# Two first-layer attentions on shared buffer rings, with the start of the second moved beside the end of the first

## The chip, the cores and the metric

The kernel runs on one core of a Trainium2 chip, in one launch. The metric is the device time of the launch in microseconds (us). Before the change three runs took 2728.13, 2721.87 and 2728.06 us; their median is 2728.06 us.

## The reference

A small vision transformer: a convolutional tokenizer turns 128 images of 128x128 into 64 tokens of 256 features each, and then two pre-norm layers follow. Only the two attentions of the first layer matter here.

```python
h = tokenizer(x)                                   # [128 images, 64 tokens, 256 features]
h = h + relu_attention(layernorm(h))               # 1: 8 heads of 32 features
h = h + expert_attention(layernorm(h))             # 2: 4 experts, 4 feature chunks, 2 heads of 32
h = h + linear_attention(layernorm(h))             # layer 1
h = h + experts(layernorm(h))                      # layer 1, gated, 8 experts

def relu_attention(x):      # a score is a small MLP over the positive part of (query - key)
    q, k, v = x @ Wq.T, x @ Wk.T, x @ Wv.T
    scores = relu(relu(q[:, None] - k[None]) @ w_mlp + b_mlp)    # per head
    return softmax(scores) @ v

def expert_attention(x):    # normalizes once more, inside
    residual = x
    xn = normalized(x) * norm_w
    gate = softmax(xn @ router_w.T + router_b)                   # over 4 experts
    q, k, v = xn[chunk] @ qkv_w[expert]
    y = softmax(q @ k.T / sqrt(32)) @ v
    y = (y @ proj_w[expert] + proj_b[expert]) weighted by gate
    return residual + y @ out_w
```

All data is fp32. The residual stream stays in SBUF for the whole first layer, in the tile `h2` of 128 partitions (2 images x 64 tokens) by 64 "pairs" of images by 256 features.

## The kernel before, in words

**First attention** (`relu_attention`, lines 290 to 757). The 128 images are cut into 8 blocks of 16 images; a block has 64 queries per image, taken 8 at a time, so there are 64 chunks (0 to 63), 8 per block. The order in which every engine gets its instructions is written out by hand (`tc.manual_schedule`): one loop body per chunk, with named places (O, X, A, V1, Y, B, W, V2, C, Z, in this order) where a dictionary `work` hangs further steps. A place belongs to one engine for the most part: O, A, B and C hold ScalarE copies, X, Y and Z matmuls, V1 and V2 VectorE steps, W GpSimd steps. In the chunk's own body VectorE makes maxima of queries and keys (L517), GpSimd makes differences (L525) that ScalarE rectifies (L526), ScalarE makes some parts alone (L535), and TensorE sums all these parts over the features of a head into the scores `sc` (L327). Beside a chunk runs the softmax of the chunk before it (VectorE L551 to L553, ScalarE L558, VectorE L561 and L562, GpSimd L565), its transpose on TensorE (L574) and the copy of that by ScalarE into the tile `at` (L582). The dictionary hangs the next block's preparation beside these chunks (statistics L347, factors L357 and L358, normalization L375, transposes L384 and L390, keys L396, values L415), and the end of the block before: `outcome`, weights times values (L471), its copies (L482), `back`, a transpose (L489), and `added`, the addition to `h2` (L499). Chunks 56 to 63 belong to the last block; no further block is prepared beside them.

After chunk 63 the last chunk's softmax and the last block's end run alone, with some idle matmuls (`c.busy`, L49) between them. Then all SBUF and PSUM pools of the first attention close.

**Second attention** (`expert_attention`, lines 760 to 1097). It opens pools of its own (L770 to L776), loads eight weight tensors (L779 to L799), multiplies two of them together (L811, kept at L819), and then runs a loop over the 64 pairs. Four pairs form a block. A block needs statistics (L834, L835), nine small GpSimd steps that make factors (`factors`, L843 to L851), per pair one GpSimd step for the normalized tile (L857) and one that normalizes `h2` in place (L860), two transposes (L865, copied at L870), router logits (L876) and their softmax (L883 to L895). In the loop these run some pairs ahead (statistics 11 and 10 pairs ahead, factors 9, transposes 4 and 3); for block 0, and in part for blocks 1 and 2, ahead means before the loop (`do("first")`, L1054, outside the manual schedule). A pair needs queries and keys (L918, copied at L922), values (L932; one half copied by ScalarE at L941, one half by VectorE with a bias at L943), scores (L954), their softmax (L966, L967, L970, L973, L974, L980, L981), the transposes of its weights (L990, L993), the product with the values (`mixed`, L1003, L1011) and the output (L1017, L1018). Every fourth pair's result leaves for DRAM (L1020). Pair p's transposes and output run in the iteration of pair p+1, and in iteration p the queries, keys and values of pair p+1 are made. Buffers: queries and keys 2, values 3, PSUM for everything but scores 4, PSUM for scores 2 of two banks each.

PSUM has 8 banks. The first attention uses 2 for scores, 2 for queries, 3 for everything else (`apq`) and 1 for the transposed weights of a chunk (`apt`); the second uses 4 for scores and 4 for the rest.

Of the kernel before, what the change touches and what calls it, by code (L numbers as in the profile page):

```python
# [1 line left out]

# [9 lines left out]
F32 = mybir.dt.float32  # L12
# [7 lines left out]
P = 128  # L20
# [269 lines left out]
def relu_attention(c, wqkv, wmlp, bmlp):  # L290
# [7 lines left out]
    NP = NB // 2  # L298
    with (
        tc.tile_pool(name="aw", bufs=1) as wp,  # L300
        tc.tile_pool(name="an", bufs=2) as np_,
        tc.tile_pool(name="ab", bufs=2) as bp,
        tc.tile_pool(name="aat", bufs=1) as atp,
# [3 lines left out]
        tc.tile_pool(name="ae", bufs=2) as ep,  # L307
        tc.tile_pool(name="aps", bufs=2, space=PSUM) as pss,
        tc.tile_pool(name="apc", bufs=2, space=PSUM) as psc,
        tc.tile_pool(name="apq", bufs=3, space=PSUM) as psq,  # L310
        tc.tile_pool(name="apt", bufs=1, space=PSUM) as pst,
    ):
        w = wp.tile([P, 2, 3 * D], F32, name="w")
# [21 lines left out]
        class Block:  # L335
# [41 lines left out]
            def transpose(self, i):  # L377

                if i == 0:
                    self.xT = bp.tile([P, 2, NP, P], F32, tag="xT", name="xT")  # L380
                self.ps["x", i] = pt = psq.tile([P, 2, 2, P], F32, tag="pq", name="pt")
                for fc in range(2):
                    for n in range(2):
                        nc.tensor.transpose(  # L384
                            pt[:, fc, n], self.xn[:, 2 * i + n, fc * P : fc * P + P], c.ident
                        )
# [5 lines left out]
            def keys(self, s, fo):  # L392

                self.ps["k", s, fo] = pk = psq.tile([P, 8, T], F32, tag="pq", name="pk")
# [15 lines left out]
            def values(self, i):  # L410

                self.ps["v", i] = pv = psq.tile([P, 2, D], F32, tag="pq", name="pv")
# [15 lines left out]
            def key_sums(self):  # L428
                self.ps["b"] = pk = psq.tile([P, T], F32, tag="pq", name="pkb")
# [34 lines left out]
            def outcome(self, hf):  # L464
                self.ps["o", hf] = po = [psq.tile([P, NP, T], F32, tag="pq", name="po") for _ in range(2)]
# [13 lines left out]
            def outcome_copied(self, hf, par):  # L479
                if hf == 0 and par == 0:  # L480
                    self.oT = np_.tile([P, 2, NP, 2, T], F32, tag="oT", name="oT", bufs=1)
                nc.scalar.copy(self.oT[:, hf, :, par], self.ps["o", hf][par])  # L482

            def back(self, i):

                self.ps["h", i] = pt = psq.tile([P, 2, D], F32, tag="pq", name="pto")
# [14 lines left out]
        class Chunk:  # L501
# [65 lines left out]
            def transpose(self):  # L567


                self.pt = pt = pst.tile([P, 8, 64], F32, tag="pt", name="pt")  # L570
# [50 lines left out]
        for b, x in enumerate(blocks):  # L621
            n = 8 * b

            at(n + 9, "X", of(x.outcome, 0))
            at(n + 9, "A", of(x.outcome_copied, 0, 0))
            at(n + 9, "B", of(x.outcome_copied, 0, 1))
            at(n + 9, "Y", of(x.outcome, 1))
            at(n + 9, "C", of(x.outcome_copied, 1, 0))
            at(n + 10, "O", of(x.outcome_copied, 1, 1))
            for i in range(4):  # L630
                at(n + 10 + i // 2, "XY"[i % 2], of(x.back, i))
                at(n + 10 + (i + 1) // 2, ("V2", "V1")[i % 2], of(x.added, i))
# [48 lines left out]
            at(n, "B", of(x.valued, 3))  # L681

# [4 lines left out]
        with tc.manual_schedule():  # L687
# [61 lines left out]
            old.exponents()  # L749
            old.sums()  # L750
            old.weights()
            c.busy(psq.tile([P, 8, T], F32, tag="pq", name="idle"), blocks[-1].k[:, 0, 0:8], 5)
            old.transpose()
            old.transposed()
            for n in range(len(seq), len(seq) + 12):
                for place in ("O", "X", "A", "V1", "Y", "B", "V2", "C", "Z"):
                    do(n, place)
        assert not work


def expert_attention(c, hd, normw, wr, br, wqkv, wvT, wproj, bproj, wout):
# [7 lines left out]
    with (  # L769
        tc.tile_pool(name="fw", bufs=1) as wp,  # L770
        tc.tile_pool(name="fb", bufs=3) as bp,
        tc.tile_pool(name="fn", bufs=2) as np_,
        tc.tile_pool(name="fv", bufs=3) as vp,
        tc.tile_pool(name="fe", bufs=4) as ep,
        tc.tile_pool(name="fps", bufs=2, space=PSUM) as pss,
        tc.tile_pool(name="fpq", bufs=4, space=PSUM) as psq,  # L776
    ):
        nw = wp.tile([P, 2], F32, name="nw")
        nc.sync.dma_start(nw, normw)  # L779
        wrs = wp.tile([P, 2, 4], F32, name="wrs")  # L780
        nc.sync.dma_start(wrs, wr.rearrange("(c p) e -> p c e", p=P))
        brs = wp.tile([P, 4], F32, name="brs")
        nc.sync.dma_start(brs, br.partition_broadcast(P))
        w = wp.tile([P, 2 * D], F32, name="w")


        bv = wp.tile([P, P], F32, name="bv")
        for k in range(2):
            nc.sync.dma_start(w[k * 64 : k * 64 + 64, :], wqkv)
            nc.sync.dma_start(  # L790
                bv[k * 64 : k * 64 + 64, :],
                bproj[2 * k : 2 * k + 2].rearrange("e o -> (e o)").partition_broadcast(64),
            )
        wv = wp.tile([32, 8, 64], F32, name="wv")
        nc.scalar.dma_start(wv, wvT)
        wpj = wp.tile([32, 8, 64], F32, name="wpj")
        nc.scalar.dma_start(wpj, wproj)
        wo = wp.tile([P, 2, D], F32, name="wo")
        nc.scalar.dma_start(wo, wout.rearrange("(c p) n -> p c n", p=P))  # L799
        eps = wp.tile([P, NB], F32, name="eps")  # L800
# [1240 lines left out]
```

## Time and profile before

| | us |
|---|---|
| median of three runs | 2728.06 |
| the profiled execution's own time | 2725.85 |
| its span (first to last instruction) | 2724.2 |
| last matmul of chunk 63 (L327) ends | at 1097.4 |
| last addition of the first attention (L499) starts its group | at 1110.7 |
| first scores of the second attention (L954), pair 0 | at 1137.46 |
| scores of pair 1 | at 1148.72 |
| scores of pair 63, the last | at 1902.09 |

Times in the trace count from the start of the span. Busy time is the time in which an engine executes at least one instruction. TensorE has two rows: PE is matmuls, PEld is the loading of weights. A matmul in fp32 shows as two records. PEclk is the granted share of TensorE's full clock. "Idle before" of a group is how long its engine stood still before its instructions, and the arrow names what ended the wait.

### The profile page before, as it was taken

How to read it: one execution, taken by the hardware profiler on the slowest of the kernel's cores; microseconds unless marked ns; L12 is line 12 of the kernel's file. 1: busy time of each engine (PE TensorE's matmuls, PEld its weight loads, DVE VectorE, ACT ScalarE, POOL GpSimd, SP SyncE). 2: the span in 40 equal slices, each digit the busy share in tenths (PEclk: the TensorE clock that was granted, in tenths of full speed). 3: DMA queues.
4: the chain of work that ended last, by engine and by line, in shares of the span. 5: the costliest groups of instructions: out<-in, count | busy, mean ns of one | idle time of the engine just before them, and what ended most of it. 6: DMA issues, size and time to landing. Idle time of an engine off the chain costs nothing. (4 is left out here: it accounts for less than half of the span.)

```text
span 2724.2 us, 80786 instructions
## 1 busy us (share of the span) xinstructions
PE 2574.9 (95%) x35209; PEld 1749.1 (64%) x35209; DVE 2023.0 (74%) x3024; ACT 1619.3 (59%) x3398; POOL 1632.4 (60%) x1386
## 2 busy tenths in 40 slices
PE   8989999999999999799999999999799996999997
PEld 4553444444444443588888888888466565888886
DVE  5759999999998999478777787877367676444443
ACT  2228888888888888466666666666255543223332
POOL 3328888888888889666566666553233312455444
PEclk9999999999999999899999999999899998999998
DMA  3100000000000000000000000000424444555554
GB/s 110 32 12 1 2 1 2 1 2 2 1 2 1 2 2 1 13 11 11 19 11 19 11 11 19 11 19 12 117 63 106 101 110 153 178 192 196 188 193 133
DMA packets 137998, 141.13 MB, mean 52 GB/s; under 512 B 107603, under 2 KB 121429, under 8 KB 129952
## 3 DMA queue, kind: packets, MB, share of 16 engines
q1 hardware_dynamic: 126896, 118.00, 14.5%
q0 software_dynamic: 7648, 14.77, 1.7%
q8 instruction: 278, 4.55, 0.7%
q10 hardware_dynamic: 3088, 3.08, 0.4%
q14 instruction: 88, 0.72, 0.1%
HBM read 104.03 MB, written 32.54 MB: 50 GB/s over the span
## 5 line engine op out<-in xcount | busy, mean ns | idle before, releaser
L525 POOL TENSOR_TENSOR m<-q,k 128x1024 f32<-128x1024 f32 x384 | 719.0, 1904 | 31.5 <-PE sc L327 16.3
L517 DVE TENSOR_TENSOR m<-pc,k 128x2048 f32<-128x2048 f32 (+1 forms) x320 | 646.8, 2058 | 0.5 <-ACT q L461 0.5
L327 PE MATMUL sc<-m,wide 128*32 128x512 f32 x4096 | 529.8, 599 | 12.0 <-DVE m L517 7.1
L526 ACT ACTIVATE m<-m 128x1024 f32<-128x1024 f32 x384 | 402.3, 1049 | 5.9 <-POOL m L525 5.4
L327 PEld LDWEIGHTS sc<-m,wide 128*32 128x32 f32 x4096 | 126.9, 109 | 259.4 <-issue 146.0
L535 ACT ACTIVATE m<-k,q 128x64 f32<-128x64 f32 x1024 | 270.9, 339 | 0.8 <-DVE k L408 0.8
L966 DVE TENSOR_REDUCE mx<-sc 128x16 f32<-128x1024 f32 x128 | 156.1, 1220 | 144.8 <-PE sc L954 142.4
L981 POOL TENSOR_TENSOR e<-e,mx 128x1024 f32<-128x1024 f32 x128 | 243.5, 1903 | 10.1 <-POOL mx L980 0.2
L922 ACT COPY qk<-pqk 128x512 f32<-128x512 f32 x256 | 139.0, 605 | 136.7 <-PE pqk L918 136.7
L980 POOL TENSOR_TENSOR mx<-mx,gate 128x16 f32<-128x16 f32 x128 | 27.6, 216 | 294.9 <-ACT z L1011 149.0
L1871 PE MATMUL ph<-xt,w1s 128*128 128x256 f32 x896 | 198.8, 380 | 3.8 <-DVE xt L1862 2.3
L1887 PE MATMUL po<-w2s,hT 128*128 128x256 f32 x896 | 198.0, 379 | 0.0
L993 ACT COPY pT<-pt 128x512 f32<-128x512 f32 x256 | 138.8, 599 | 92.1 <-PE pt L990 92.1
L1871 PEld LDWEIGHTS ph<-xt,w1s 128*128 128x128 f32 x896 | 170.0, 190 | 28.2 <-DVE xt L1862 3.0
L1887 PEld LDWEIGHTS po<-w2s,hT 128*128 128x128 f32 x896 | 168.3, 190 | 21.5
L918 PE MATMUL pqk<-xT,w 64*128 64x128 f32 x2048 | 169.9, 289 | 3.7 <-issue 3.5
L967 DVE TENSOR_TENSOR e<-sc,mx 128x1024 f32<-128x1024 f32 x128 | 156.8, 1225 | 4.4
L1905 POOL DMA_INDIRECT out<-y,rout x56 | 56.7, 1013 | 167.8 <-ACT hT L1875 124.8
L918 PEld LDWEIGHTS pqk<-xT,w 64*128 64x128 f32 x2048 | 142.3, 189 | 21.8 <-issue 11.8
L973 DVE TENSOR_REDUCE mx<-e 128x16 f32<-128x1024 f32 x128 | 153.2, 1197 | 1.8 <-ACT e L970 1.8
L990 PE MATMUL pt<-ident,e 128*128 128x128 f32 x1024 | 144.0, 281 | 11.1 <-DVE v L943 5.1
L1875 ACT ACTIVATE hT<-ph,w1s 128x256 f32<-128x256 f32 x224 | 93.0, 470 | 96.9 <-PE ph L1871 96.9
(298 smaller groups left out, 4926.5 us busy)
## 6 DMA issues: line engine op xcount, KB each, us to landing
w1s<-in_we SPq DMA_DIRECT2D x30, 1028.0 KB, 5.1
w2s<-in_we SPq DMA_DIRECT2D x30, 1024.0 KB, 4.9
hd<-h SPq DMA_DIRECT2D x16, 512.0 KB, 3.2
x<-hd SPq DMA_DIRECT2D x16, 512.0 KB, 3.8
h<-hd SPq DMA_DIRECT2D x4, 2048.0 KB, 13.2
hx<-h SPq DMA_DIRECT2D x4, 2048.0 KB, 11.6
out<-h SPq DMA_DIRECT2D x4, 2048.0 KB, 20.5
xt<-in_x SPq DMA_DIRECT2D x15, 512.0 KB, 3.6
```

The lines of the kernel that those rows point to most:

```text
L327: nc.tensor.matmul(dst[j : j + 32], wide[:, hf, s : s + 32], part, start=start, stop=stop)
L517: nc.vector.tensor_tensor(m, bcast(self.pq[:, hf, i : i + n], 3, T), k, ALU.max)
L525: nc.gpsimd.tensor_tensor(m, bcast(self.q[:, hf, s : s + 2], 3, T), k, ALU.subtract)
L526: nc.scalar.activation(m, m, AF.Relu)
L535: nc.scalar.activation(self.parts[i, hf][:, q], self.blk.k[:, hf, i], AF.Relu, bias=self.q[:, hf, i - NB // 2, q : q + 1], scale=-1.0,)
L918: nc.tensor.matmul(pq[par][:, k, eh, :], w[r, f : f + P], self.xT[r, fc], start=True, stop=True)
L966: nc.vector.tensor_reduce(mx, sc, AX.X, ALU.max)
L967: nc.vector.tensor_sub(e, sc, bcast(mx, 2, T))
L973: nc.vector.tensor_reduce(self.sm[x], self.e[x], AX.X, ALU.add)
L981: nc.gpsimd.tensor_mul(e, e, bcast(sm, 2, T))
L1871: nc.tensor.matmul(ph[:, j], self.w1[:, w0 : w0 + P], self.xt[:, fc], start=(fc == 0), stop=(fc == 1))
L1887: nc.tensor.matmul(po, self.hT[:, f, r * P : r * P + P], self.w2[:, f, :], start=(f == 0), stop=(f == 7))
```

## The change

1. A class `Shared` holds the pools that both attentions use: one ring of 4 PSUM banks for everything but scores and queries (in the first attention it takes the place of the 3 of `apq` and the 1 of `apt`), and the SBUF rings of the first attention. The second attention has no SBUF pools of its own but for softmax tiles (`fe`); it takes slots of the first's rings: queries and keys from the ring `k`, values from the ring `v` (2 slots, where its own had 3), weights from a slot of `xT`, and three "rows" (`xn`, the other `xT`, `oT`), each of which holds a block's normalized tile in one half and its transpose in the other.
2. `expert_attention` is called first; it returns a dictionary `beside` of steps and a function `rest`. `relu_attention` hangs the steps of `beside` into its chunks: statistics of the second attention's blocks 0, 1 and 2 beside chunks 43 to 48; factors of blocks 0 and 1, cut in four parts each, beside 45 to 52; the weights' loads at 55 and 57, now all on SyncE's queue; the product of two of them at 58; block 0's normalization, on ScalarE (`normal_scalar`) where GpSimd did it, at 58 and 59; its transposes, logits and gates at 59 to 63; queries, keys and values of pair 0 at 61 to 63. The small loads of `normw`, the router's weight and bias move to the start of the first attention.
3. The end of the last chunk and of the last block no longer runs before the second attention. A function `first` writes out the order of pair 0 by hand, with the last chunk's softmax and transpose, `outcome`, `back` and `added` among pair 0's own steps; two of the outcome's four copies go to VectorE. The in-place normalization of block 0 (`stream`) comes last in it on GpSimd, that of block 1 beside pairs 2 and 3. The idle matmuls are gone.
4. From pair 1 on the loop is as before, but for block 2, whose factors come two pairs later than its distance would have them (at pair 1) and whose normalization comes at pairs 1, 2, 3 and 3.

```diff
+class Shared:
+    def __init__(self, c, ctx):
+        self.np_, self.bp = pool("an", 2), pool("ab", 2)
+        self.atp, self.ep, self.small = pool("aat", 1), pool("ae", 2), pool("as", 1)
+        self.psq = pool("apq", 4, space=PSUM)
...
-        tc.tile_pool(name="apq", bufs=3, space=PSUM) as psq,
-        tc.tile_pool(name="apt", bufs=1, space=PSUM) as pst,
...
+        for (n, place), steps in beside.items():
+            at(n, place, *steps)
...
             old.less_max()
-            old.exponents()
-            old.sums()
-            old.weights()
-            c.busy(psq.tile([P, 8, T], F32, tag="pq", name="idle"), blocks[-1].k[:, 0, 0:8], 5)
-            old.transpose()
-            old.transposed()
-            for n in range(len(seq), len(seq) + 12):
-                for place in ("O", "X", "A", "V1", "Y", "B", "V2", "C", "Z"):
-                    do(n, place)
+    return old, blocks[-1]
...
+    def ring(pool, tag, shape, **k):
+        t = pool.tile(shape, F32, tag=tag, name=f"{tag}r", **k)
...
+        def load(self):
+            row = ring(sh.bp, "xT", [P, 2, 8, P])
...
+        def load_values(self):
+            for k, x in enumerate((wvT, wproj)):
+                y = sh.w[0:32, k, D : 3 * D].rearrange("p (e n) -> p e n", e=8)
+                nc.sync.dma_start(y, x)
...
+        def offsets(self):
+            g.tensor_mul(self.nb, self.mv[:, 0:NB, 0], self.ra)
+            g.tensor_scalar(self.nb, self.nb, -1.0, None, ALU.mult)
...
+        def stream(self, n):
+            nc.gpsimd.tensor_scalar(hn, hn, self.rs[:, i], self.mr[:, i], ALU.mult, ALU.subtract)
+        def normal_scalar(self, n):
+            nc.scalar.activation(self.xn[:, n, :], hn, AF.Identity, bias=self.nb[:, i], scale=self.ra[:, i])
...
-                self.qk = vp.tile([P, 4, 2, 2, P], F32, tag="qk", name="qk", bufs=2)
-                self.v = vp.tile([P, 2, 2, 4, P], F32, tag="v", name="v")
+            qk = ring(sh.bp, "k", [P, 2, 16, T])
...
+                v = ring(sh.bp, "v", [P, 8, D])
...
-            at(n - 9, "POOL", x.factors)
+        if b > 1:
+            at(n - 9 + 2 * (b == 2), "POOL", x.factors)
             for k in range(NB):
-                at(n - 8 + k, "POOL", x.normal, k)
+                at(min(n - 8 + k + (b == 2), n - 5), "POOL", x.normal, k)
+        elif b == 1:
+            for k in range(NB):
+                at(2 + k // 2, "POOL", x.stream, k)
...
+    for k, blk in enumerate((x, y, z)):
+        for i in range(2):
+            by(43 + 2 * k + i, "V2", blk.statistics, 2 * i)
+    for k, blk in enumerate((x, y)):
+        for i in range(4):
+            by(45 + 4 * k + i, "W", blk.factors, (i,))
+        by(48 + 4 * k, "W", blk.offsets)
+    by(55, "Z", wt.load)
+    by(57, "Z", wt.load_values)
+    for n, place, k in ((58, "C", 0), (58, "C", 1), (59, "A", 2), (59, "B", 3)):
+        by(n, place, x.normal_scalar, k)
+    by(58, "Z", wt.values)
+    by(59, "V1", wt.kept)
+    by(59, "Z", x.transpose, 0)
+    by(60, "A", x.transposed, 0)
+    by(60, "Z", x.transpose, 1)
+    by(61, "O", x.transposed, 1)
+    by(61, "X", x.logits)
+    by(61, "V2", x.logits_less_max)
+    by(62, "A", x.exponents)
+    by(63, "V1", x.sums)
+    by(63, "W", x.gates)
+    by(61, "Z", pair, "queries_keys", 0)
+    by(62, "O", pair, "queries_keys_copied", 0)
+    by(62, "X", pair, "queries_keys", 1)
+    by(62, "V2", pair, "queries_keys_copied", 1, nc.vector.tensor_copy)
+    by(62, "Z", pair, "values", 0)
+    by(63, "O", pair, "values_kept", 0)
+    by(63, "X", pair, "values", 1)
+    by(63, "V1", pair, "values_kept", 1)
+
+    def first(cur, new, chunk, last):
+        new.queries_keys(0)
+        chunk.exponents()
+        new.queries_keys_copied(0)
+        chunk.sums()
+        chunk.weights()
+        cur.scores()
+        cur.less_max(0)
+        y.normal_scalar(0)
+        new.queries_keys(1)
+        cur.less_max(1)
+        chunk.transpose()
+        new.queries_keys_copied(1)
+        chunk.transposed()
+        cur.exponents(0)
+        last.outcome(0)
+        last.outcome(1)
+        for par in range(2):
+            last.outcome_copied(0, par)
+        cur.sums(0)
+        cur.weights(0)
+        cur.exponents(1)
+        for par in range(2):
+            last.outcome_copied(1, par, nc.vector.tensor_copy)
+        cur.sums(1)
+        cur.weights(1)
+        new.values(0)
+        new.values_kept(0)
+        last.back(0)
+        last.back(1)
+        last.added(0)
+        last.added(1)
+        for k in range(1, 4):
+            y.normal_scalar(k)
+        new.values(1)
+        new.values_kept(1)
+        last.back(2)
+        last.back(3)
+        last.added(2)
+        last.added(3)
+        for k in range(NB):
+            x.stream(k)
+        do((0, "POOL"))
+        do((0, "PE"))
```

## The prediction

> **What bounds the kernel now.** I read the page's head first, then the row of each engine in stages cut at the change (the view of windows), then the groups of two chunks, and last the timeline of the passage from the first attention to the second. The page's own chain of waits is of no use here: it stops at the last output.
>
> ```profile
> span 2724.2 us, 80786 instructions
> ```
>
> ```profile
> 1097.40:1137.46 40.06, 27.37 (x471) 20.85 (x467) 11.50 (x39) 8.18 (x15) 24.29 (x35) 0.74 0.08 20
> 673.54:787.11 113.57, 112.43 (x1245) 48.81 (x1227) 106.54 (x106) 99.81 (x225) 99.82 (x59) 1.00 0.01 2
> 1063.60:1088.23 24.63, 24.63 (x216) 8.62 (x212) 24.28 (x21) 21.77 (x50) 24.42 (x15) 1.00 0.01 2
> 1148.72:1902.00 753.28, 736.77 (x19453) 655.84 (x19452) 595.95 (x861) 474.46 (x851) 444.04 (x493) 1.00 0.05 14
> ```
>
> The columns are length, then busy time of PE, PEld, DVE, ACT and POOL, granted TensorE clock, DMA. Row two is eight chunks with a block's preparation beside them (from one L558 to the eighth after it), row three two late chunks without: 12.31 us each, so a block's side work costs 113.57 - 8 x 12.31 = 15.1 us. Row four is the pairs, 753.28 / 62 = 12.15 us each, with TensorE full. Row one is the passage: 40.06 us in which VectorE and ScalarE are almost idle and TensorE has 0.74 of its clock.
>
> ```profile
> L525 POOL TENSOR_TENSOR m<-q,k 128x1024 f32<-128x1024 f32 x13 | 24.3, 1904 | 0.0
> L517 DVE TENSOR_TENSOR m<-pc,k 128x2048 f32<-128x2048 f32 (+1 forms) x11 | 22.4, 2079 | 0.0
> L327 PEld LDWEIGHTS sc<-m,wide 128*32 128x32 f32 x128 | 4.1, 109 | 11.2 <-issue 5.5 <-ACT m L526 3.4 <-DVE m L517 1.9
> ```
>
> In the two late chunks VectorE and GpSimd never stand still before their main work (last column 0.0): they set the pace. TensorE's weight loads wait 5.3 us for ScalarE and VectorE.
>
> ```profile
> 1095.55 1.94 PE L327 MATMUL sc<-m,wide 128*32 128x512 f32 x16
> 1097.41 4.56 PE L49 MATMUL idle<-k,ident 128*128 128x512 f32 x10
> 1097.54 0.70 DVE L551 TENSOR_REDUCE pc<-sc 128x8 f32<-128x512 f32 x1 [3.02 <-PE sc L327]
> ...
> 1104.26 1.50 PE L471 MATMUL po<-at,v 64*32 64x64 f32 x130 [0.68 <-ACT at L582]
> ...
> 1110.69 2.48 DVE L499 TENSOR_TENSOR h<-h,pto 128x512 f32<-128x512 f32 x4
> ...
> 1114.69 2.09 PE L811 MATMUL pwv<-wpj,wv 32*64 32x64 f32 x32 [2.60 <-DVE st L834]
> ...
> 1117.17 2.44 POOL L857 TENSOR_SCALAR xn<-h,mv,ra 128x256 f32<-128x256 f32 x2
> ...
> 1125.01 0.69 ACT L870 ACTIVATE xT<-ptx,nw 128x512 f32<-128x512 f32 x1 [14.95 <-PE ptx L865]
> ...
> 1127.69 3.15 PE L876 MATMUL pg<-wrs,xT 128*128 128x4 f32 x14
> ...
> 1134.26 2.08 PE L918 MATMUL pqk<-xT,w 64*128 64x128 f32 x16
> ...
> 1137.46 1.59 PE L954 MATMUL sc<-qk 32*64 32x64 f32 x128
> ```
>
> ```profile
> 1148.72 1.59 PE L954 MATMUL sc<-qk 32*64 32x64 f32 x128
> ...
> 1162.37 1.16 PE L918 MATMUL pqk<-xT,w 64*128 64x128 f32 x16
> ...
> 1170.85 1.84 PE L876 MATMUL pg<-wrs,xT 128*128 128x4 f32 x16
> ```
>
> The passage is one chain: the last softmax and block end to 1110, statistics, factors on GpSimd, normalization on GpSimd (1117 to 1125), transposes, logits, queries. Sixteen records of L918 take 2.08 us in it and 1.16 later: its matmuls also run at the slow clock. Pair 1's scores start at 1148.72, which is **51.3 us** after chunk 63's last matmul (1097.4). From there on both kernels do the same work, so I compare at this point.
>
> **What goes, and what takes its place.** In the new order, let 0 be the end of chunk 63's last matmul. TensorE does pair 1's first queries to 1.2. The last chunk's maximum and subtraction (L551 to L553) end at 1.7; they free the PSUM banks that pair 0's scores take. Scores 1.75 to 3.35. Then VectorE is the long engine: two times L966 and L967 (2.45 each), the chunk's sums (0.9), two sums L973 and L974 (2.9), two copies of 128x512 (0.69 each, as L819), L943 (1.22), four additions L499 (2.7). With the 1.7 at the start that is 17.2 us. TensorE has 2 x 1.16 + 1.59 + 1.15 + 2 x 1.50 + 2.1 + 4 x 0.6, some 12.6 us, with waits for the softmax (weights on GpSimd end at 4.5, copy into `at` at 6.3, outcome to 9.4), and cannot do block 1's transpose before the second half of the additions has freed PSUM, about 15.9. Then 0.6 for that and 1.1 for pair 0's first transposes: pair 1's scores at 17.5 at the earliest. I take 18.5, since every step here waits on another engine, and 21.5 as the late end (half again of TensorE's work at a clock that dips: in the stretch 1900 to 1920, where TensorE is busy 15.06 of 20 us, the profile grants 0.83). So the passage gives back 51.3 - 18.5 = **32.8 us** (29.8 to 33.8). The idle matmuls that go hid nothing but the clock.
>
> **What is paid beside chunks 58 to 63.** From the warm rows of the pair loop: transposes 2 x 0.60, logits 1.84, queries and keys 2 x 1.16, values 2.11, and the product of weights, half of its 2.09 at the slow clock: 8.5 us of TensorE. The rows where this work stood sum to 16.8, at a clock of 0.6 to 0.7; beside chunks the clock is 1.00, so I take 8.5. ScalarE: four normalizations (0.60 each, L375), two L870 (0.69), gates 0.2, two copies of queries and two of values (1.07 the two): 6.1. VectorE: 0.69, logits 0.5, sums 0.35, two copies 1.4, L943 1.22: 4.2. GpSimd 0.2. That is 19 us of engine time. A block's own side work is the nearest row: by its groups TensorE 25.1, ScalarE 14.0, VectorE 8.4, GpSimd 2.0, together 49.5 us, which cost 15.1, or 0.30 us for one. 19 x 0.30 = **6 us**. At least 3, since VectorE has no idle time there and 4.2 come to it; at most 8.5 + 4.2 = 12.7. Here the Trainium skill ("Perfetto Trace Analysis", Identifying the Most-Contended Engine) bears: matmul busy time is no measure of TensorE's room, the share of weight loading is. Row three has 24.63 of 24.63 busy in matmuls but 8.62, 35%, in loads, and its loads wait for others. Read by busy time, TensorE is full and the 8.5 us are paid whole (10 to 13 us in all); by the rule most hide. I go with the rule, as the waits of L327 agree. What is queued behind an inserted step: behind ScalarE's copies at O the parts for TensorE's next sums; behind VectorE's copies at V2 of chunk 62 chunk 63's first maxima, and TensorE waits for these.
>
> **What is paid beside 43 to 52.** Statistics: 12 x (0.40 + 0.17) = 6.8 us of VectorE. Factors: 7 x 0.2 + 2 x 1.02 and offsets 0.4 per block, 7.7 us of GpSimd. The eight stretches from the exponential at 814.47 to that at 927.37 have one block's statistics and a part of its factors less than the eight at 700.91 to 814.47, some 6 us of engine time, and take 112.9 instead of 113.6: 0.1 for one. By that 1.7 us, by the block's ratio 4.4; **3 us**, 0 to 7. A rule speaks against this part: the Trainium skill ("GPSIMD Engine Reference", Key points) says that GpSimd shares its SBUF interfaces with VectorE and contends with its two-input or two-port instructions. If all statistics held GpSimd up, 6.8 us would come on top. The trace shows none of it: L525 takes 1897 to 1913 ns in all 384 cases, beside whatever VectorE does. I take nothing for it.
>
> **The pair loop.** At pair 3 GpSimd now gets two normalizations of block 2 (4.9), block 1's last two in-place steps (2.5) and block 3's factors (3.4) after its weights: 10.8 us against a gap of about 7.5 to pair 4's weights. 3 us late; TensorE has half of it as slack: **1.5 us** (0 to 3). `v` has 2 slots for 3, at nothing: the product with the old values stands just ahead of the new values on TensorE (L1003, 2.09, then L932), so the slot is free before the copy comes. One PSUM ring of 4 for 3 + 1: each slot is asked for four allocations later, when its copy is done; nothing. The loads go on SyncE, which has nothing else before the first result leaves; three small loads ahead of `wide` move it by about 1.3 us, and it is first needed at 198.2, over 10 us after its issue.
>
> **Sum.** 32.8 - 6 - 3 - 1.5 = 22.3 us. The profiled execution took 2725.85 us, 2.2 under the median of the runs (2721.87 to 2728.13): 2725.85 - 22.3 = **2703.5, say 2704 us**. Ends: 33.8 - 3 = 30.8 gives 2695; 29.8 - 12.7 - 7 - 3 = 7.1 gives 2719.
>
> **The rivals.** *Better cover* (0.14): statistics and factors free, only VectorE paid at the end: 2695. For it, the 0.1 above; against, VectorE and GpSimd's zero idle time. *Little cover* (0.14): every insertion breaks the hand-written order, matmuls are paid one for one: about 2719. For it, the PE row at 100%; against, the waits. *A new wait in every pair* (0.05), the one that makes it slower: the copy of values waits for its slot in the ring of 2. It decides from 22.3 / 63 = 0.35 us per pair; if the copy slipped behind the output's matmuls (L1017, 1.13 us), 63 x 1.13 = 71 us, and 2704 + 71 = 2775. For it, TensorE is the bound in row four, so any slip counts; against, the order named above. *The change doesn't do what it says* (0.05): the new pools `fe` and the scores' PSUM lie where the first attention's were, and if they waited for its very end, pair 0's scores would still stand behind it, at about 1110.69 + 2.48 = 1113.2 instead of 1137.46: 24.3 less the 10.5 paid is 13.8, or 2712.
>
> **How the numbers follow.** The forecast has 0.62, by itself 2697 to 2712. The range 2695 to 2718 takes in most of both neighbours. 0.3%, about what a measurement of this kernel tells from no change, is 8.2 us: under 2719.9 counts as faster. Forecast 0.62, better cover 0.14, the last rival 0.05 and half of little cover make 0.88 faster; its other half 0.07 within; slower 0.05.
>
> **What would show it.** Pair 1's scores 17.5 to 21.5 us after the last L327; late chunks 58 to 63 longer by 6 us together, 44 to 52 by 3; pairs still at 12.15 us; granted clock near 1.00 through the passage. I am wrong if the pairs grow by 0.3 us or the late chunks by over 12.

## The result, and the profile after

The changed kernel takes **2709.53 us**, the median of five runs (2703.53 to 2711.76), beside 2727.61 us (2721.87 to 2728.13) for the kernel before on the same chip: a ratio of 0.9938, with a 95% interval from 0.9921 to 0.9954. It is faster by about 18 us. The forecast was 2704 us, with a range from 2695 to 2718.

The profiled execution took 2711.76 us, the longest of the five. Line numbers have moved: L327 is now L340, L517 is L530, L525 is L538, L551 is L564, L918 is L987 and L954 is L1034.

```profile
span 2710.0 us, 80818 instructions
```

These are the four stages that answer to those of before, in the same view and with the same columns:

```profile
675.03:788.60 113.57, 112.41 (x1243) 48.74 (x1226) 106.54 (x106) 99.82 (x225) 99.81 (x59) 1.00 0.01 2
1070.30:1097.48 27.18, 27.18 (x319) 13.04 (x320) 26.05 (x26) 23.94 (x55) 25.21 (x16) 1.00 0.01 2
1108.20:1127.40 19.20, 15.77 (x672) 13.36 (x670) 14.87 (x22) 11.06 (x19) 8.18 (x8) 1.00 0.01 3
1125.80:1886.54 760.74, 740.29 (x19454) 658.71 (x19453) 596.61 (x861) 475.25 (x851) 454.73 (x508) 1.00 0.05 14
```

Eight early chunks take 113.57 us, as before: the shared rings cost them nothing. The two late chunks take 27.18 us instead of 24.63, and TensorE's weight loads in them are busy 13.04 us instead of 8.62: that is the work that came in. The passage (row three) runs from the last sum to pair 1's first maximum. Before the change the same stretch was this:

```profile
1097.48:1150.29 52.81, 36.97 (x833) 28.96 (x832) 21.44 (x51) 15.04 (x26) 35.24 (x52) 0.81 0.06 16
```

It is now little over a third as long, with all five engines at work and TensorE at its full clock. The pairs from 1 to 63 take 760.74 us, 7.4 more than before, where the forecast had 1.5.

TensorE's timeline through the passage (start, duration, what ran, and the idle time before it):

```profile
1106.21 2.01 PE L340 MATMUL sc<-m,wide 128*32 128x512 f32 x16
1108.15 1.16 PE L987 MATMUL pqk<-xnr,xTr 64*128 64x128 f32 x16
1110.12 1.58 PE L1034 MATMUL sc<-kr 32*64 32x64 f32 x128 [0.80 <-DVE e L566]
...
1114.69 1.96 PE L484 MATMUL po<-at,v 64*32 64x64 f32 x175 [0.68 <-ACT at L595]
1118.46 1.04 PE L484 MATMUL po<-at,v 64*32 64x64 f32 x81 [1.80 <-issue]
...
1125.80 1.59 PE L1034 MATMUL sc<-kr 32*64 32x64 f32 x128
```

Pair 1's scores stand at 1125.80, 17.6 us after the last sum's end at 1108.2; before, it was 51.2 us. One can now set up the account of this one execution against the profiled one of before:

| step | us |
|---|---|
| tokenizer and first 43 chunks | +1.5 |
| stretches of chunks 43 to 57 | +2.3 |
| from there to the last sum of chunk 63 | +7.0 |
| last sum to the first maximum of pair 1 | -33.7 |
| pair 4 to pair 5, against 11.4 before | +5.3 |
| other pairs | +2.1 |
| after the last pair | +1.4 |
| sum (the spans, 2724.2 and 2710.0, give -14.2) | -14.1 |

The first line and the last two can't be put down to the change. Over the 14 traces here, with nearly the same instructions in these parts, the first exponential of the first attention comes anywhere from 215.2 to 219.9 us, the other pairs together take 739.5 to 744.1 us, and what follows the last pair 817.8 to 822.3. Without those three lines the change is worth 19.1 us, close to the 18.1 between the medians.

### The profile page after: what moved, and what is told of

Same layout as the page of the kernel before. It is cut to its first block, busy times and chain, and to the rows that moved or that the text cites. A ratio compares the mean times of both kernels' runs of the same rounds, so it can differ in the third digit from the quotient of the medians.

```text
span 2710.0 us, 80818 instructions
## 1 busy us (share of the span) xinstructions
PE 2564.6 (95%) x35199; PEld 1743.5 (64%) x35199; DVE 2028.0 (75%) x3028; ACT 1622.6 (60%) x3402; POOL 1623.4 (60%) x1382
## 5 line engine op out<-in xcount | busy, mean ns | idle before, releaser
L538 POOL TENSOR_TENSOR m<-q,k 128x1024 f32<-128x1024 f32 x384 | 718.8, 1903 | 28.8 <-PE sc L340 14.3
L530 DVE TENSOR_TENSOR m<-pc,k 128x2048 f32<-128x2048 f32 (+1 forms) x320 | 647.2, 2058 | 0.5 <-ACT q L474 0.5
L340 PE MATMUL sc<-m,wide 128*32 128x512 f32 x4096 | 528.4, 599 | 14.1 <-DVE m L530 8.9
L340 PEld LDWEIGHTS sc<-m,wide 128*32 128x32 f32 x4096 | 126.2, 109 | 254.7 <-issue 140.7
L993 ACT COPY kr<-pqk 128x512 f32<-128x512 f32 x254 | 137.9, 603 | 137.2 <-PE pqk L987 137.1
L1060 POOL TENSOR_TENSOR mx<-mx,gate 128x16 f32<-128x16 f32 x128 | 27.6, 216 | 297.3 <-ACT z L1091 129.4
L2076 ACT ACTIVATE y<-y,gf 128x256 f32<-128x256 f32 x56 | 28.0, 506 | 195.7 <-issue 107.1
L1050 ACT ACTIVATE e<-e 128x1024 f32<-128x1024 f32 x128 | 139.6, 1091 | 2.5 <-DVE e L1047 2.5
## 6 DMA issues: line engine op xcount, KB each, us to landing
h<-hd SPq DMA_DIRECT2D x4, 2048.0 KB, 12.7
```

Source lines behind the costliest of these rows:

```text
L340: nc.tensor.matmul(dst[j : j + 32], wide[:, hf, s : s + 32], part, start=start, stop=stop)
L530: nc.vector.tensor_tensor(m, bcast(self.pq[:, hf, i : i + n], 3, T), k, ALU.max)
L538: nc.gpsimd.tensor_tensor(m, bcast(self.q[:, hf, s : s + 2], 3, T), k, ALU.subtract)
```

## The experiments

Each is an edit of the changed kernel. In what follows "passage" is the time from the end of chunk 63's last sum to pair 1's first maximum: 52.8 us before, 19.1 after.

### What costs 5 us at pair 5: GpSimd's queue

GpSimd's timeline of the changed kernel, between pair 3's weights and pair 4's (L1060), and below it TensorE's at the same time:

```profile
1162.89 2.42 POOL L923 TENSOR_SCALAR h<-h,rs,mr 128x256 f32<-128x256 f32 x2
1165.28 0.22 POOL L964 TENSOR_TENSOR gate<-gate,gm 128x16 f32<-128x16 f32 x1
1165.48 1.23 POOL L916 TENSOR_SCALAR oTr<-h,mv,rs 128x256 f32<-128x256 f32 x1
1166.81 1.23 POOL L923 TENSOR_SCALAR h<-h,rs,mr 128x256 f32<-128x256 f32 x1
1168.02 1.23 POOL L916 TENSOR_SCALAR oTr<-h,mv,rs 128x256 f32<-128x256 f32 x1
1169.35 1.23 POOL L923 TENSOR_SCALAR h<-h,rs,mr 128x256 f32<-128x256 f32 x1
1170.55 0.20 POOL L889 TENSOR_TENSOR rs<-mv,eps 128x4 f32<-128x4 f32 x1
...
1174.43 0.22 POOL L1060 TENSOR_TENSOR mx<-mx,gate 128x16 f32<-128x16 f32 x1
1174.72 1.90 POOL L1061 TENSOR_TENSOR e<-e,mx 128x1024 f32<-128x1024 f32 x1
```

```profile
1172.50 0.60 PE L934 MATMUL ptx<-ident,oTr 128*128 128x128 f32 x4
1176.68 1.97 PE L1070 MATMUL pt<-ident,e 128*128 128x128 f32 x8 [3.58 <-POOL e L1061]
1178.58 2.26 PE L1034 MATMUL sc<-kr 32*64 32x64 f32 x128
1180.77 2.08 PE L987 MATMUL pqk<-xTr 64*128 64x128 f32 x16
```

Two in-place steps of block 1 (L923, both in the first row), a gate, two normalizations of block 2 and the factors of block 3 (L889 to L901) stand in a row. Each normalization is two steps here: L916 for the normalized tile, then L923 again, in place, for the same pair of block 2. Together this is 11.5 us, from 1162.89 to 1174.43, although VectorE's reciprocal for the first half of pair 4's weights had been ready since 1170.4. So GpSimd comes 4.0 us late. TensorE waits 3.58 us for the weights, and its next three groups then run slowly, at a granted clock of 0.50: 1.97, 2.26 and 2.08 us, where the rows below show 1.04, 1.59 and 1.16. So the stall costs twice: once in the wait, once in the clock. The first experiment takes block 1's in-place steps from pairs 2 and 3 to pairs 4 to 7, one each, and moves the third of block 2's four normalizations from pair 3 to pair 2:

```diff
-                at(min(n - 8 + k + (b == 2), n - 5), "POOL", x.normal, k)
+                at((1, 2, 2, 3)[k] if b == 2 else n - 8 + k, "POOL", x.normal, k)
-                at(2 + k // 2, "POOL", x.stream, k)
+                at(4 + k, "POOL", x.stream, k)
```

> Edit against the changed kernel: block 1's in-place steps on GpSimd go beside pairs 4 to 7 (were 2, 2, 3, 3), block 2's normalizations beside 1, 2, 2, 3 (were 1, 2, 3, 3). Theory A (GpSimd's queue at pair 3 is the cause): in the changed kernel pair 5's first maximum comes 16.7 us after pair 4's, where the kernel before has 11.4; with 3.6 us less queued at pair 3, GpSimd reaches pair 4's weights in time, the step is 11.4 to 12.5 us again, and the kernel is 4 to 5.3 us faster than the changed one. Rival B (the stall is a data or PSUM wait that only shows there, or comes back at the pair where the steps now stand): no gain, within 1 us, or the same stall at pairs 4 to 8.

It took **2701.9 us** (2699.83 to 2703.32), ratio 0.9910 (0.9893 to 0.9927). Its GpSimd and TensorE timelines at the same pair:

```profile
1161.25 1.23 POOL L916 TENSOR_SCALAR oTr<-h,mv,rs 128x256 f32<-128x256 f32 x1
1162.58 1.23 POOL L923 TENSOR_SCALAR h<-h,rs,mr 128x256 f32<-128x256 f32 x1
1163.77 0.20 POOL L889 TENSOR_TENSOR rs<-mv,eps 128x4 f32<-128x4 f32 x1
...
1168.67 0.22 POOL L1060 TENSOR_TENSOR mx<-mx,gate 128x16 f32<-128x16 f32 x1 [0.97 <-ACT z L1091]
```

```profile
1170.68 0.60 PE L934 MATMUL ptx<-ident,oTr 128*128 128x128 f32 x4
1171.12 1.04 PE L1070 MATMUL pt<-ident,e 128*128 128x128 f32 x8
1172.08 1.59 PE L1034 MATMUL sc<-kr 32*64 32x64 f32 x128
1173.60 1.16 PE L987 MATMUL pqk<-xTr 64*128 64x128 f32 x16
```

At pair 3 the edit took 4.9 us out of GpSimd's queue (two in-place steps and a normalization of two steps), not the 3.6 of the expectation; what each of the two moves does alone was not tried. GpSimd is free 0.97 us before it is asked, TensorE doesn't wait at all, and pair 4 to 5 takes 11.4 us, as before the change. This is no matter of one trace: with this edit pair 4 to 5 takes 11.4 us in all four traces of this document, and without it 15.7 to 16.8 us in all nine traces of changed versions. The pairs from 1 to 63 took 752.8 us here, the value of before: the rest of the loop carries no cost from the change. This version is faster than both kernels; measured beside the changed one on the same chip (below), it lies 4.5 us under it.

### What the interleaving with pair 0 is worth

The next edit undoes part 3 of the change alone: the last softmax and the last block's end run first, then pair 0.

```diff
-        new.queries_keys(0)
         chunk.exponents()
...
+        last.outcome(0)
+        last.outcome(1)
...
+        for k in range(4):
+            last.back(k)
+            last.added(k)
+        new.queries_keys(0)
```

> Edit: the last chunk's softmax and the last block's end run alone again, ahead of pair 0; block 0's preparation stays beside the chunks. Theory A (the interleaving of pair 0 is worth a good part of the 33.7 us of the passage): the end takes about 14 to 16 us as in the kernel before (1097.4 to 1113), pair 0 to pair 1's scores 11 us, so pair 1's scores come 25 to 27 us after the last sum of chunk 63 instead of 17.6: 8 to 10 us slower than the changed kernel, a third of the passage's gain. Rival B (the moved preparation alone gives it; pair 0's steps only wait for each other while the end runs beside them): within 3 us of the changed kernel.

2721.58 us (2718.07 to 2728.13), ratio 0.9986 (0.9978 to 0.9994): most of the gain is gone. The chunks grew exactly as in the changed kernel; the passage took 34.0 us, 14.9 longer, which is more than expected. In the view of windows this version's passage had a clock of 0.70:

```profile
1107.00:1141.00 34.00, 22.10 (x672) 18.72 (x668) 15.13 (x21) 11.34 (x19) 7.12 (x7) 0.70 0.01 2
```

To part order from clock, nine idle matmuls were put back into the waits of this version (five after the last chunk's weights, one after the outcome's copies, three after pair 0's values):

```diff
         chunk.weights()
+        c.busy(ps([P, 2, D], "idle"), h2[:, 0:2], 5)
...
         new.values_kept(1)
+        c.busy(ps([P, 2, D], "idle"), h2[:, 0:2], 3)
```

> Edit: as e3_end_first (the end of the first attention alone, ahead of pair 0), with nine idle matmuls of 128x512 (0.86 us each) in its three longest waits of TensorE. In e3_end_first pair 1's first maximum came 34.0 us after the last sum and the granted clock in this stretch was 0.70, in the changed kernel 19.1 us and 1.00. Theory A (the slow clock is a part of the loss, by the rows some 6 us: the transposes of back 3.5 for 1.9, outcome 3.6 for 3.0, scores 1.8 and 2.3 for 1.6, and so on): the clock is above 0.9 and the stretch 27 to 30 us, so that the interleaving itself is worth 8 to 11 us. Rival B (the chain of engines sets the stretch and the clock is hidden in it): 33 to 34 us again, at a clock near 1.00.

The passage of this kernel in the same view:

```profile
1104.75:1134.22 29.47, 23.49 (x688) 16.89 (x688) 14.87 (x22) 11.13 (x19) 6.52 (x7) 1.00 0.01 2
```

It took 29.5 us at the full clock. So in the traces 10.3 us of the loss (29.5 less 19.1) is order, work of two stages that no longer overlaps, and 4.6 us is clock. The medians do not carry the second number: 2720.99 us (2715.44 to 2723.54) beside 2721.58. That the idle matmuls raise this passage's clock is seen in one trace each, and no more.

### What the work beside the chunks costs and brings

All of part 2 of the change is undone: the steps of `beside` run in a row after chunk 63 (the exact order of their places kept).

```diff
-        for (n, place), steps in beside.items():
-            at(n, place, *steps)
...
             old.less_max()
+            for key in sorted(beside, key=lambda k: (k[0], order.index(k[1]))):
+                for step in beside[key]:
+                    step()
```

> Edit: all steps that the change hangs beside chunks 43 to 63 run in the same order right after chunk 63, rings and pair 0's interleaving as in the change. Theory A (rings cost nothing; what the steps cost beside chunks is 9 to 10 us, what they cost alone is 20 to 25): the chunk lengths are those of the kernel before to 0.1 us, pair 1's scores come some 40 us after the last sum, and the kernel is 10 to 16 us slower than the changed one, near the kernel before. Rival B (shared PSUM ring or the extra waits in it slow the chunks): chunks before 43 or after 53 are longer than in the kernel before.

2721.0 us (2718.17 to 2722.88), ratio 0.9978 (0.9970 to 0.9986). Every stretch from chunk 42 to 63 but one (0.15 us shorter) is within 0.01 us of its length before the change. So all 9.3 us that the chunks lose belong to the steps, and none to shared rings. The passage took 42.0 us, 22.9 longer, at a clock of 0.80:

```profile
1099.20:1141.30 42.10, 30.75 (x825) 26.61 (x822) 24.37 (x56) 16.87 (x30) 15.86 (x31) 0.80 0.01 2
```

In the traces the steps save 22.9 us for 9.3 paid, a part of the 22.9 being clock. By the medians this version is 5.3 us faster than the kernel before, where the changed kernel was 18.1.

**Chunks 43 to 57.** Of their 2.3 us, 1.06 and 0.80 fall in the first two stretches with statistics. Before the change, these two and the next read:

```profile
814.47:828.05 13.58, 13.58 (x117) 5.49 (x110) 13.40 (x14) 12.58 (x28) 12.18 (x9) 1.00 0.01 2
828.05:843.69 15.64, 14.79 (x115) 5.38 (x115) 13.81 (x13) 12.56 (x29) 14.28 (x9) 1.00 0.01 2
843.69:858.34 14.65, 14.65 (x118) 6.28 (x117) 12.24 (x11) 12.55 (x29) 12.53 (x8) 1.00 0.00 1
```

and after it:

```profile
815.96:830.60 14.64, 14.64 (x122) 5.65 (x118) 14.40 (x18) 12.58 (x28) 13.24 (x9) 1.00 0.01 2
830.60:847.03 16.43, 14.48 (x112) 4.99 (x105) 15.58 (x17) 12.56 (x28) 13.21 (x9) 1.00 0.00 0
847.03:861.68 14.65, 14.65 (x118) 6.27 (x117) 13.22 (x15) 12.67 (x28) 12.71 (x9) 1.00 0.00 1
```

In the first, VectorE (third busy time) is busy 13.40 of 13.58 us: 1.0 us of statistics makes the stretch 1.06 longer. In the third, it has 2.4 us to spare, and the same statistics cost 0.00. The second does not fit this: VectorE had 1.8 us to spare there, and the stretch still grew by 0.80; why stays open. A move by two chunks should drop most of the cost:

```diff
-            by(43 + 2 * k + i, "V2", blk.statistics, 2 * i)
+            by(45 + 2 * k + i, "V2", blk.statistics, 2 * i)
-            by(45 + 4 * k + i, "W", blk.factors, (i,))
-        by(48 + 4 * k, "W", blk.offsets)
+            by(47 + 4 * k + i, "W", blk.factors, (i,))
+        by(50 + 4 * k, "W", blk.offsets)
```

> Edit: statistics beside chunks 45 to 50 instead of 43 to 48, factors and offsets beside 47 to 54 instead of 45 to 52. In the changed kernel chunks 43 and 44 grew by 1.06 and 0.80 us, the price of two statistics each, and the other eight by 0.4 together. Theory A (those two chunks have no idle VectorE time, the others have): the whole added time of the stretch falls from 2.3 to about 0.5 us. Rival B (the first statistics that come are paid wherever they stand, since the engines' lead over each other is used up once): 2.3 us again, now at chunks 45 and 46.

One run took 2706.85 us. The first two stretches cost 0.0; two later ones 0.40 (chunk 49) and 0.38 (chunk 51), and the sum to chunk 57 was 1.05 us instead of 2.27. The 0.38 is not the move's: the changed kernel pays 0.35 there, too. Nor does the 0.40 seem to be: the changed kernel has -0.15 at chunk 49 in one trace and +0.05 in another, and in two further traces with the statistics where this edit puts them (below) it is -0.15 and the sum 0.44. So the move saves about 1.8 us. What the statistics cost is decided by the chunk beside which they stand; VectorE's spare time tells most of it, but not all.

**Chunks 58 to 63.** They grow by 1.84, 0.59, 0.51, 1.38, 1.18 and 1.49 us. The first is the product of the two weights. TensorE's timeline after, and then VectorE's maximum in that stretch before and after (last column: idle before, and for whom):

```profile
1038.06 1.89 PE L829 MATMUL pwv<-w 32*64 32x64 f32 x32
```

```profile
L551 DVE TENSOR_REDUCE pc<-sc 128x8 f32<-128x512 f32 x1 | 0.7, 691 | 0.0
```

```profile
L564 DVE TENSOR_REDUCE pc<-sc 128x8 f32<-128x512 f32 x1 | 0.7, 700 | 1.7 <-PE sc L340 1.7
```

The product takes 1.89 us just ahead of the chunk's last sums, and the next maximum waits 1.7 us for them, where it waited 0.0 before. Two edits move this work, and one doubles it. The first starts the normalizations a chunk earlier and spreads them:

```diff
-    for n, place, k in ((58, "C", 0), (58, "C", 1), (59, "A", 2), (59, "B", 3)):
+    for n, place, k in ((57, "C", 0), (58, "A", 1), (58, "B", 2), (59, "A", 3)):
```

> Edit: ScalarE's four normalizations of block 0 at 57 C, 58 A, 58 B, 59 A (were 58 C twice, 59 A, 59 B). In the changed kernel the stretch from the end of chunk 58 into 59 grew by 1.84 us. Theory A (the product of weights, 1.89 us on TensorE just ahead of the chunk's last sums, is paid one for one): 1.7 to 1.9 us again. Rival B (the two normalizations ahead of ScalarE's next parts are what is paid, 1.2 us): the growth falls to 0.7 us, with at most 0.6 coming in one chunk earlier.

2709.18 us, one run: the stretch grew by 2.32, and one before it by 0.49. It got worse by 1 us: starting the normalizations earlier does not lower the 1.84.

The second puts product, transposes and first queries at Y, before the chunk's later sums, instead of Z, and the normalizations at 57 C and 58 A, B and C (lines that the excerpt leaves out):

```diff
-    by(58, "Z", wt.values)
+    by(58, "Y", wt.values)
-    by(59, "Z", x.transpose, 0)
+    by(59, "Y", x.transpose, 0)
...
-    by(61, "Z", pair, "queries_keys", 0)
+    by(61, "Y", pair, "queries_keys", 0)
```

> Edit: TensorE's product of weights, both transposes and the first queries of pair 0 stand at place Y of chunks 58 to 61, where the chunk's next sums wait for ScalarE and VectorE (in the changed kernel 0.5 to 1.4 us at a time), and not at Z, ahead of the chunk's last sums; ScalarE's normalizations at 57 C and 58 A, B, C. The stretch from chunk 57 to the last sum grew by 7.0 us in the changed kernel, over 8.6 us of added TensorE work. Theory A (the place decides, what stands in a wait is hidden): 3 to 4.5 us. Rival B (TensorE's work is paid wherever it stands, since its waits there are the lead of the other engines over it): 6.5 to 7.5 us.

2706.5 us, one run: the stretches grew by 0.49, 1.90, 0.39, 0.06, 1.55, 1.17 and 1.47, again 7.0 in all. The sum did not fall. But this edit moves two things, and earlier normalizations alone cost 1 us in the edit above; so place Y may have hidden about 1 us of TensorE's work, which this run can't tell.

Last, the product is computed twice:

```diff
-            for k in range(2):
+            for k in (0, 1, 0, 1):
```

> The product of the two weight tensors beside chunk 58 is computed twice over, the second time into the same place; nothing else changes. Theory A (TensorE's work in a late chunk is paid one for one, as stretch 57's growth of 1.84 us beside a product of 1.89 us says): that stretch grows by a further 1.9 us, to 3.7. Rival (the first product fell into a hole of the order, and what hides it is used up only in part, or the growth belongs to the loads and normalizations beside it): a further 0 to 0.9 us.

2715.42 us, one run. The product took 3.40 us, 1.51 longer, and the stretch 3.35 more than before the change, also 1.51 longer; VectorE's wait in it:

```profile
L564 DVE TENSOR_REDUCE pc<-sc 128x8 f32<-128x512 f32 x1 | 0.7, 700 | 3.3 <-PE sc L340 3.3
```

So the second product, too, is paid one for one, for the time that it really adds. (Most of the rest of this run's loss is its passage: 22.6 us, of which 6.8 us were at half clock.)

### The best version, and what a clock does to a verdict

Both improvements together, the spread in-place steps and the later statistics:

> The fastest of the versions put together: block 1's in-place steps one per pair, the statistics two chunks later, the factors two chunks later. Theory A (two separate costs, each with its own place): both gains add, the pairs 4 to 5 take 11.4 us instead of 16.7 and chunks 43 to 57 grow by about 1.0 us instead of 2.3, so the median is 1.2 us below that with the pairs' edit alone: about 2700.5 us, ratio about 0.9905. Theory B (what the later statistics save at the chunks comes back in the next stretches or in pair 0): chunk growth up to the last sum as in the changed kernel, 10 to 11 us, and a median of 2702 or more.

2699.65 us (2698.79 to 2702.33), ratio 0.9907 (0.9891 to 0.9924). The chunks from 43 on grew by 7.4 us instead of 9.3, so they saved 1.8 us, more than expected; but the passage took 20.35 us, and gave 1.2 back. The edits with later statistics and with the normalizations apart had shown 20.2 and 20.1, too. Was that the kernel's order? Three versions were run once more, side by side:

> The changed kernel once more, for a second trace of the passage. Theory A (the length of the passage belongs to the kernel: its order gives its clock): 19.1 us again from the last sum to pair 1's first maximum, at a granted clock of 1.00, and 16.7 us for pair 4 to 5. Theory B (the clock in the passage differs from execution to execution of one kernel): 20 us or more, at a clock under 0.95. The median about 2709.

> The version with block 1's in-place steps spread, beside the next one on the same chip. Theory A: passage 19.1 us at clock 1.00 again; median 2702. Theory B: the passage may come out at 20 us.

> The version with statistics two chunks later as well. Theory A (its passage is slower because of its place in time): 20.3 us at a clock of about 0.87 to 0.94 again, so what the statistics save, 1.2 us, is given back, and the median equals that of the version without the shift within 0.5 us. Theory B (the clock of the passage was chance): 19.1 us in this trace, or 20 in the others too, and a median 1.2 us below that of the version without the shift.

The medians are 2707.1 us for the changed kernel (2706.38 to 2708.72; ratio 0.9927, 0.9913 to 0.9941), 2702.63 with the steps spread (2700.91 to 2705.54; 0.9911, 0.9896 to 0.9927), and 2700.66 with both (2697.29 to 2705.35; 0.9908, 0.9892 to 0.9924). Here are two stretches of the last version's passage, in its first trace and then in its second, each divided where the granted clock can change (more on that in the last section):

```profile
1111.81:1115.23 3.42, 1.24 (x123) 1.09 (x113) 2.09 (x3) 2.03 (x3) 1.00 (x2) 1.00 0.02 5
1115.23:1118.64 3.41, 3.41 (x84) 2.91 (x79) 2.58 (x4) 0.66 (x2) 1.12 (x1) 0.50 0.02 5
```

```profile
1109.49:1112.90 3.41, 1.50 (x150) 1.35 (x137) 2.47 (x3) 2.12 (x4) 0.61 (x2) 1.00 0.02 5
1112.90:1116.31 3.41, 3.34 (x112) 2.48 (x95) 2.66 (x5) 1.63 (x4) 1.51 (x1) 1.00 0.03 5
```

The same order of instructions fell once so that matmuls filled 1.24 us of the first stretch, and the next ran at half clock; the other time it was 1.50 us, and the clock stayed. The passage took 20.35 and 19.40 us. These two traces come from two chips, but all ten traces with this order of the passage agree: with no time at half clock it takes 19.1 to 19.4 us (six traces), with 3.41 us of it 20.1 to 20.4 (three), with 6.83 us 22.6 (one). So the passage's clock is an execution's, and what the version with both saves stays saved. Measured beside each other, its median lies 2.0 us below that without the shift, and its chunks grew by 1.9 us less. The expected 1.2 came from the one trace with 0.40 at chunk 49. The runs' ranges overlap, so by the times alone the sign is likely and the size open. In the changed kernel's second trace pair 4 to 5 took 15.7 us instead of 16.7; over all nine traces the stall is 4.2 to 5.4 us.

## Why the prediction was right, step by step

The forecast's mechanism held, and one of its terms failed. It lies 5.5 us under the median. Its sum was 22.3 us where the account gives 19.1: the passage came out 0.9 us and the statistics 0.7 us better than forecast, the late chunks 1.0 and the pair loop 3.8 us worse, so the errors cancel in part. And it was set off from the profiled execution of before, 1.8 us under that kernel's median on this chip.

- **The passage**: forecast 32.8 us given back, with scores at 17.5 us at the earliest and 18.5 taken. They came at 17.6, and 33.7 us were given back. The clock was 1.00 here, as said, but 0.85 to 0.92 in four of the ten traces with this order. That 17.6 meets the 17.5 is luck in part. The items listed for VectorE add up to 15.7 us, not to 17.2, and it was not the long engine all the way: from the last sum to pair 1's scores it was busy 14.8 of 17.6 us, TensorE 14.2 (forecast at 12.6), and TensorE had hardly a pause in the last 7.3 us.

```profile
1108.22:1125.80 17.58, 14.15 (x542) 11.81 (x541) 14.83 (x21) 10.37 (x18) 6.58 (x7) 1.00 0.01 4
```

- **Chunks 58 to 63**: forecast 6 us (3 to 12.7), measured 7.0. One item was mis-sized: the product was priced at half of its 2.09 us, as if these had been at half clock. The profile grants 0.85 in that stretch (1114.69 to 1116.78), so most of it ran at the full clock, and beside chunk 58 it takes 1.89. The forecast weighed the row of matmuls against the rule of the Trainium skill ("Perfetto Trace Analysis", Identifying the Most-Contended Engine), which judges TensorE's room by MFU (the share of the peak rate) and by the share of weight loading; the forecast used the second alone. The result lies between the two readings: by the timeline 9.7 us of TensorE's work was added (product 1.89, transposes 1.32, logits 1.95, queries 2.32, values 2.20), and 7.0 us were paid, neither most hidden nor all. In the two late chunks of the profile 5.6 us were added and 2.55 paid; what hid the rest were the loads' waits for ScalarE and VectorE, which the forecast had pointed at: 5.3 us of them before, 1.6 after (0.4 and 1.2 in the row below). The product was paid whole: it stands between a chunk's sums, of which the last release VectorE's next maximum, and the 1.8 us of such waits in its stretch lay elsewhere and stayed (1.6 after). The 0.30 us per us of engine time gave nearly the right sum, but not for its reason.

```profile
L340 PEld LDWEIGHTS sc<-m,wide 128*32 128x32 f32 x132 | 4.0, 108 | 5.9 <-issue 3.1 <-DVE m L530 1.2 <-ACT m L539 0.4
```

- **Chunks 43 to 52**: forecast 3 us, measured 2.3. The Trainium skill's rule cited there ("GPSIMD Engine Reference", Key points) names VectorE instructions in a 2-port mode or with two SBUF inputs; a statistics instruction reads one tile (`st<-h`), so the second does not apply, and its mode no run shows. No hold-up is seen: L538 averages 1903 ns over the kernel, as L525 had 1904.
- **The pair loop**: forecast 1.5 us (0 to 3), measured 4.2 to 5.4: the **failed term**. The forecast saw the right place and the right queue: it counted 10.8 us where 11.5 stood, against a gap of 7.5 us (1162.89 to 1170.4), so GpSimd was 4.0 us late instead of 3. What it had wrong is the rest: TensorE's slack took about 0.4 us of the lateness, not half, for TensorE waited 3.58 us; and there was nothing in the sum for the half clock that came with that wait.
- **Rings, loads, start**: forecast at nothing, and nothing in the early chunks or, with the steps spread, in the pairs.

None of the rivals came about. The new wait in every pair would have shown in the mean pair. Without pair 4 to 5, this is 12.20 us in the changed kernel's trace and 12.17 in its second, 12.16 with the steps spread and 12.16 before. The pools' wait for the first attention's end did not exist: pair 0's scores start at 1110.12, before the last block's end. *Better cover* is refuted by 9.3 us paid beside the chunks. *Little cover* has about three quarters of TensorE's added work on its side, but not the statistics (2.3 us), and its 2719 lies above every run.

## What to carry to other kernels

Hanging a start and an end of stages beside each other's work pays well when neither fills an engine (here 34 us from the passage for 9 beside the chunks), but read the engine's spare time in each stretch: the same statistics cost 1.06 us in one and nothing two chunks on. After such a move, look for the steps that were pushed out of the way: in-place steps and normalizations in GpSimd's queue, ahead of weights that TensorE needed, took back 4 to 5 us, and an edit of two lines that spread them gave these again. Judge differences of 1 us in a passage by several traces, since its clock alone makes as much.

## What the runs showed of the hardware

**The clock changes in steps of 3.41 us.** In all 14 traces, each stretch that the profile grants at half clock lasts 3.41 us or a whole multiple of it (up to 20.48 us), but for those in which the kernel ends. The grid on which the clock changes lies differently in each execution. Here are the stretches around pair 4's wait in the changed kernel's two traces, divided on this grid (matmuls' busy time first, clock third from the end):

```profile
1172.57:1175.98 3.41, 0.54 (x5) 0.29 (x3) 0.69 (x2) 0.69 (x1) 3.10 (x7) 1.00 0.45 154
1175.98:1179.39 3.41, 2.71 (x61) 2.38 (x67) 0.00 (x0) 1.17 (x2) 3.33 (x4) 0.50 0.00 0
1179.39:1182.80 3.41, 3.41 (x112) 3.07 (x102) 1.89 (x2) 0.00 (x0) 1.83 (x2) 0.50 0.02 5
```

```profile
1173.72:1177.14 3.42, 1.49 (x50) 1.33 (x53) 0.00 (x0) 0.74 (x2) 3.34 (x3) 1.00 0.30 102
1177.14:1180.55 3.41, 3.41 (x115) 3.23 (x110) 1.76 (x2) 0.33 (x1) 3.05 (x3) 0.50 0.03 5
1180.55:1183.96 3.41, 3.41 (x59) 3.01 (x56) 3.15 (x4) 3.14 (x6) 0.00 (x0) 1.00 0.01 2
```

The wait was 3.58 us in the first trace and 3.57 in the second, but 6.83 us at half clock came with the one (from 0.7 us before its end) and 3.41 after the other, and pair 4 to 5 took 16.7 and 15.7 us. In the first, three groups took 6.31 us where they take 3.79, which is 2.5 us on top of the wait. Between 300 and 1900 us the 14 traces have 32 changes from full to half clock. Each follows a stretch of the grid with at most 1.65 us of matmuls; where the full clock stayed, the stretch had at least 1.48 us.

The Trainium skill ("TensorE: Matmul & The Clock Gate", Part 1: The HAM clock gate) says that the clock halves after an idle window of about 3.4 us, and that these windows run freely and do not start anew with a kernel. The length, the half and the free running agree with these traces. That the window has to be idle does not: one with 1.49 us of matmuls was enough.

**Not all matmuls halve with the clock.** The pair's queries (16 records of 64x128) take 1.16 us at the full clock and 2.08 at half. Its scores (128 records of 32x64) take 1.59 us at the full clock and 2.26 at 0.50, 1.4 times as long and not twice.
